# Attention with its largest scores taken ahead, and 3x3 depthwise convolutions shared between TensorE and VectorE

## The chip, the cores and the metric

The kernel runs on one core of a Trainium2 chip. A core has five engines that run on their own and wait for one another by semaphores: TensorE (PE, with its weight loads as PEld), VectorE (DVE), ScalarE (ACT), GpSimd (POOL) and SyncE (SP), whose queue issues most transfers. PE writes its results to PSUM, eight banks of 128 x 512 f32[...]. The metric is the device time of one execution in microseconds (us). The time before is 16835.43 us, the median of three runs (16829.09 to 16853.61).

## The reference

A network of four layers on an input of 4 batches x 96 channels x 56 x 56; each layer adds its result for the normalised input (groups of three channels) to the input.

- Layer 0: attention over all 3136 positions with three heads of 16 channels; softmax over all positions, projection to 96 channels.
- Layer 1: input projection to 192 channels, a 3x3 depthwise convolution, SiLU, and a selective scan along eight paths over the picture (rows, columns and two diagonals, each both ways); the eight results are merged, normalised, gated and projected.
- Layer 2: for each position the eight most similar positions in a window, a weighted mean of them, and a feed-forward net.
- Layer 3: again projection and depthwise convolution, a cumulative recurrence in four directions, a gate, and then a bottleneck: 1x1 convolution to 384 channels, affine and ReLU, a 3x3 depthwise convolution, affine and ReLU, 1x1 convolution to 96, and a squeeze gate over the channels.

For the change, these lines matter:

```python
attn = jnp.einsum('bhnd,bhmd->bhnm', q, k) * scale
attn = jax.nn.softmax(attn, axis=-1)
out = jnp.einsum('bhnm,bhmd->bhnd', attn, v)
...
xc = lax.conv_general_dilated(xc, conv_w, (1, 1), 'SAME', feature_group_count=DI, ...)
xc = jax.nn.silu(xc + conv_b[None, :, None, None])
...
t = jax.nn.relu(bn(conv2d(t, c2_w, c2_b, groups=2 * E, pad=1), bn2_g, bn2_b, bn2_m, bn2_v))
```

## The kernel before

All data are f32. A matmul of f32 leaves two records in the trace[...].

**Layer 0** (`layer0`, L113 to L341). The 3136 positions are cut into 7 chunks of 448 columns (`NCH`, `CH`) and 25 tiles of 128 rows (`NT`, the last of 64). A head has 16 channels, padded to 32, so that the four batches lie in the four strips of 32 partitions (`rows[b]`). `project` (L171) makes queries and keys of one head for one chunk, `values` (L155) the values.

The softmax needs the largest score of each query first. A **unit** (head, tile of queries, chunk of keys) computes the scores (`scores`, L197) of 128 queries against 448 keys for each batch, and `largest` (L210) reduces each on DVE to one maximum per query. When the seven chunks of a tile are done, `of_tile` (L218) takes the maximum of the seven, and `into_row` (L227, L229) turns it into a row and subtracts it within the queries, in a channel that is kept for it. A **step** (head, chunk of 448 queries, tile of 128 keys) then computes the transposed scores (`weigh`, L237), takes the exponential on ACT (`exps`, L246), and sums values and weights in `gathered` (L255): for each batch a matmul over 128 keys into a strip of 32 partitions of one PSUM bank `acc`. After 25 steps, `finish` (L260) copies `acc` (L264), turns the denominators into rows (L267, L269), takes reciprocals in four parts (L273) and multiplies; for the last head it also multiplies by the output weights (L287), adds bias and input (L291) and writes the chunk out (L292).

The order is written out by hand: `in_order` (L53) makes each engine follow the program's order. There are 525 units and 525 steps. 32 units (`LEAD`) go ahead of the first step. Then each step does, twice: weigh two batches, score the other two for a unit, exponentials of the first two (one instruction each), maxima of the other two, sums of the first two. So units and steps advance at one rate, and the last 32 steps have no unit. PSUM: four banks for `weigh` (`psE`), three for everything else (`psM`, `bank()`), one for `acc`.

**Convolutions.** `into_scan` (L344, layer 1), `into_layer3` (L938) and `bottleneck` (L1412, within `layer3`) each fill a padded tile of 128 channels x 58 x 58 (`xp`, `t1`): a projection on PE in seven chunks, each copied by ACT (L385, L972, or with affine and ReLU L1426). `depthwise` (L418) then runs nine instructions on DVE over the whole tile of 128 x 3136: the first multiplies (L423), the others multiply and add in place (L425). ACT applies SiLU or affine and ReLU to the whole tile (L391, L978, L1433). In `into_scan` the result is written to DRAM in four orders: rows as it is; columns through a transposing copy on ACT (L403); the two diagonals through a doubled copy `dup` (ACT L394 and POOL L395) and two gathering copies on POOL (L405, L407). `into_scan` and `into_layer3` have six tiles each (two pairs of batches x three), the bottleneck three for each of four batches. There is no order by hand here; the tile framework places instructions by their dependencies. A pair's inputs are loaded through one buffer `x` (L365, L957) and normalised just before its tiles.

Layer 3's output alternates for each batch between `gathered` (L1374: loads the four directions' results, sums, normalises, gates) and `bottleneck`. Their SBUF pools are opened and closed in turn, so they use the same places: `ob`, `os` for the one, `tb`, `t1`, `ts` for the other.

**Between them** lie the scans (L427 on), layer 1's output, layer 2 and the cumulative sums (L989 on), which the diff doesn't touch.

Of the kernel before, what the change touches and what calls it, by code (L numbers as in the profile page):

```python
# [17 lines left out]
L = H * W  # L18
# [51 lines left out]
class Net:  # L70
# [42 lines left out]
    def layer0(self, xin, xout):  # L113


        nc, tc = self.nc, self.tc
# [4 lines left out]
        LEAD = 32  # L121
        with ExitStack() as cx:
# [4 lines left out]
            psE = cx.enter_context(tc.tile_pool(name="l0pE", bufs=4, space=PSUM))  # L127
# [27 lines left out]
            def values(b, t0):  # L155
                some = n128[t0 : t0 + 8]
                n = some[0][1]
                p = psE.tile([128, 512], F32, name="s")
                for i, (k0, nk) in enumerate(some):
                    nc.tensor.matmul(  # L160
                        p[:nk, i * 48 : (i + 1) * 48], xns[b][:, k0 : k0 + nk], wv, start=True, stop=True
                    )
                nc.scalar.copy(
                    va[:n, t0 : t0 + len(some), :, b, 0:HD],
                    p[:n, : 48 * len(some)].rearrange("p (t h d) -> p t h d", h=HEADS, d=HD),
                )
# [23 lines left out]
            def scores(u, bs):  # L190

                h, t, kc = u
                q0, nq = n128[t]
                ps = []
                for b in bs:
                    p = bank()
                    nc.tensor.matmul(  # L197
                        p[:nq, :CH], qas[h][rows[b], q0 : q0 + nq],
                        kas[h][rows[b], kc * CH : (kc + 1) * CH], start=True, stop=True,
                    )  # L200
                    ps.append(p)
                return ps

            def largest(u, bs, ps):
# [4 lines left out]
                for b, p in zip(bs, ps):  # L209
                    nc.vector.tensor_reduce(  # L210
                        pms[h, t][:nq, b : b + 1, kc], p[:nq, :CH], AX.X, ALU.max
                    )

            def of_tile(u):

                h, t, _ = u
# [5 lines left out]
            def into_row(u):  # L222

                h, t, _ = u
# [6 lines left out]
            def weigh(s, bs):  # L231
# [3 lines left out]
                for b in bs:  # L235
                    p = sc[s, b] = psE.tile([128, 512], F32, name="s")
                    nc.tensor.matmul(  # L237
                        p[:nk, :CH], kas[h][rows[b], k0 : k0 + nk],
# [3 lines left out]
            def exps(s, bs):  # L242
                nk = n128[s[2]][1]
                for b in bs:
                    e = ss.tile([128, CH], F32, name="e", bufs=8)
                    nc.scalar.activation(e[:nk], sc[s, b][:nk, :CH], AF.Exp, scale=scale)  # L246
                    sc[s, b] = e

            def gathered(s, bs):
                h, qc, t = s  # L250
                nk = n128[t][1]
                if t == 0 and bs[0] == 0:
                    sc["acc"] = psA.tile([128, 512], F32, name="acc")
                for b in bs:
                    nc.tensor.matmul(  # L255
                        sc["acc"][rows[b], :CH], va[:nk, t, h, b, :], sc[s, b][:nk],
                        start=t == 0, stop=t == NT - 1,
                    )

            def finish(h, qc):  # L260
# [23 lines left out]
                for b in range(B):  # L284
                    p = bank()
                    for i in range(HEADS):
                        nc.tensor.matmul(  # L287
                            p[:C, :CH], wo[rows[b], i, :], aos[i][rows[b], cs],
                            start=i == 0, stop=i == HEADS - 1,
                        )  # L290
                    nc.vector.scalar_tensor_tensor(xs[b], p[:C, :CH], bo, xs[b], ALU.add, ALU.add)  # L291
                    nc.gpsimd.dma_start(xout[b][:, cs], xs[b])  # L292
                    yield

            with in_order(tc):
                for c in range(NCH):
                    project(0, c)
                parts = [(b, t0) for t0 in range(0, NT, 8) for b in range(B)]
                sc = {}
                at_u = 0  # L300
                ended = None
                done = iter(())
                for at in range(-LEAD, len(steps)):
                    u = units[at_u] if at_u < len(units) else None
                    at_u += 1
                    s = steps[at] if at >= 0 else None
                    new = steps[at + 1] if -1 <= at < len(steps) - 1 else None
                    if s is None and parts:
                        values(*parts.pop(0))
                    for two, first in (((0, 1), True), ((2, 3), False)):  # L310
                        other = (2, 3) if first else (0, 1)
                        if new is not None:
                            weigh(new, two)
                        if u is not None:
                            ps = scores(u, other)
                        if new is not None:
                            exps(new, two)
                        if u is not None:
                            largest(u, other, ps)
                        if s is not None:  # L320
                            gathered(s, two)
                    if ended is not None:
                        into_row(ended)
                        ended = None
                    if u is not None and u[2] == NCH - 1:
                        of_tile(u)
                        ended = u
                    next(done, None)
                    if s is None:
                        continue  # L330
                    h, qc, t = s
                    if qc == 0 and t == 0:
                        aos.append(s1.tile([128, L], F32, name=f"ao{h}", **({"tag": "xn0"} if h == 2 else {})))
                    if t == NT - 1:
                        done = finish(h, qc)
                        next(done)
                    r = at % (NCH * NT) - (NCH * NT - LEAD - 5 * NCH)
                    if h < HEADS - 1 and r >= 0 and r % 4 == 0 and r < 4 * NCH:
                        project(h + 1, r // 4)
                for _ in done:  # L340
                    pass  # L341


    def into_scan(self, xin, dram, orders):  # L344
# [3 lines left out]
        us = []  # L348
        xs = [dram.tile([C, L], F32, name=f"l1x{b}") for b in range(B)]
        with ExitStack() as cx:  # L350
# [8 lines left out]
            for pr in range(NPAIR):  # L359
                u = [dram.tile([128, NB, L], F32, name=f"l1u{pr}{o}") for o in orders]  # L360
                us.append(dict(zip(orders, u)))
                xn = []
                for half in range(2):
                    x = s1.tile([C, L], F32, name="x")
                    nc.sync.dma_start(x, xin[2 * pr + half])  # L365
                    xh = s1.tile([C, L], F32, name=f"xn{half}")
                    self.group_norm(x, xh, ss, ps, "p")
                    nc.sync.dma_start(xs[2 * pr + half], xh)
                    xn.append(xh)

                def project(col, c):
                    p = ps.tile([128, 512], F32, name="p")
                    for half in range(2):
                        nc.tensor.matmul(
                            p[64 * half : 64 * half + 64, :CH], win[:, col : col + 64],
                            xn[half][:, c * CH : (c + 1) * CH], start=True, stop=True,
                        )
                    return p

                for j in range(NB):  # L380
                    xp = sp.tile([128, H + 2, W + 2], F32, name="xp")
                    self.pad_border(xp)
                    for c in range(NCH):
                        p = project(64 * j, c)
                        nc.scalar.copy(  # L385
                            xp[:, 1 + 8 * c : 9 + 8 * c, 1 : W + 1],
                            p[:, :CH].rearrange("p (h w) -> p h w", w=W),
                        )
                    cv = sp.tile([128, H, W], F32, name="cv")
                    self.depthwise(cv, xp, cw[:, j, :])  # L390
                    nc.scalar.activation(cv, cv, AF.Silu, bias=cb[:, j : j + 1])  # L391

                    dup = sp.tile([128, H, 2 * W], F32, name="dup")
                    nc.scalar.copy(dup[:, :, 0:W], cv)  # L394
                    nc.gpsimd.tensor_copy(dup[:, :, W : 2 * W], cv)  # L395
                    for o in orders:
                        dst = us[pr][o][:, j, :]
                        if o == "rows":
                            nc.sync.dma_start(dst, flat(cv))
                            continue  # L400
                        t = sp.tile([128, W, H], F32, name="t")
                        if o == "cols":
                            nc.scalar.copy(t, view(cv, 0, [[1, W], [W, H]]))  # L403
                        elif o == "diag":
                            nc.gpsimd.tensor_copy(t, view(dup, 0, [[1, W], [2 * W + 1, H]]))  # L405
                        else:
                            nc.gpsimd.tensor_copy(t, view(dup, W, [[1, W], [2 * W - 1, H]]))  # L407
                        nc.sync.dma_start(dst, flat(t))
        return us, xs

    def pad_border(self, xp):
        nc = self.nc
        nc.gpsimd.memset(xp[:, 0, :], 0.0)
# [1203 lines left out]
```

## Time and profile before

| | us |
|---|---|
| median of three runs | 16835.43 |
| profiled execution, its own time | 16926.37 |
| its span | 16924.6 |
| layer 0, to the last output products | 0 to 2439 |
| of which: lead of 32 units / loop with units / rest | 66 to 228 / 236 to 2240 / to 2439 |
| into_scan, to the first scan | 2440 to 2797 |
| scans | 2797 to 9286 |
| layer 1's output, layer 2 | 9293 to 10932 |
| into_layer3 | 10933 to 11215 |
| cumulative sums | 11225 to 16122 |
| layer 3's output, of which a bottleneck some 124 | 16131 to 16915 |

The profile is that of one execution. Its page gives each engine's busy time and share, the span in 40 slices with the busy tenths of each engine and the clock granted to TensorE, and groups of instructions by line. PE's busy time counts pipelined matmuls with modelled ends, so a busy PE is not one at its peak; start-to-start distances on its timeline tell more. A stretch gives the same for a chosen part of the span. The share of the span that the chain of waits spends on lines of this change: PE s L237 6%, PE acc L255 6%, DVE cv L425 3%, PE m L197 1%.

### The profile page before, as it was taken

The numbers are of one execution on the slowest core, as the hardware profiler recorded it, in microseconds if no ns is written. First come the engines' busy times: TensorE is split into PE (matmuls) and PEld (weight loads), VectorE is DVE, ScalarE is ACT, GpSimd is POOL, SyncE is SP. The second block draws the span as 40 slices with busy tenths as digits, with TensorE's granted clock in tenths as the row PEclk, the third lists the DMA queues.
The fourth block names the chain that finished last, engine by engine and source line by source line (L and its number), as shares of the span: only waits on it lengthen the run. The fifth ranks groups of instructions, "written<-read, shape, count | busy, mean of one in ns | idle before, by whom it ended". The sixth has DMA issues, their size and how long they took to land.

```text
span 16924.6 us, 498034 instructions
## 1 busy us (share of the span) xinstructions
PE 13192.5 (78%) x220632; PEld 8680.7 (51%) x220632; DVE 14110.1 (83%) x14839; ACT 12324.2 (73%) x16300; POOL 7670.4 (45%) x4010
## 2 busy tenths in 40 slices
PE   8999983777777777777777677738888888888844
PEld 3222222666666666666665545426665656666622
DVE  5666637999999999999999678768888888888887
ACT  2555435999999999999998235448888888888812
POOL 0000005888888888888887000013333333333300
PEclk7999976999999999999999578869999999999966
DMA  0000004334444443434444910032221222222122
GB/s 14 1 1 1 14 27 149 92 90 95 97 102 107 105 95 93 94 90 103 106 101 98 221 48 6 21 79 50 50 50 48 50 50 50 50 50 49 45 64 66
DMA packets 821388, 1152.29 MB, mean 68 GB/s; under 512 B 309360, under 2 KB 728720, under 8 KB 807456
## 3 DMA queue, kind: packets, MB, share of 16 engines
q1 hardware_dynamic: 760320, 1060.20, 25.8%
q10 hardware_dynamic: 53536, 40.96, 1.1%
q8 instruction: 1734, 28.41, 0.7%
q0 software_dynamic: 5376, 19.27, 0.4%
q14 instruction: 422, 3.46, 0.1%
HBM read 842.93 MB, written 277.18 MB: 66 GB/s over the span
## 4 chain that ended last, share of the span: by engine, by line
PE 31%; DVE 28%; ACT 18%; issue 17%; DMA 3%; POOL 2%; SPq 0%; DVEq 0%; ACTq 0%; POOLq 0%
DVE q L555 16%; PE q L1248 6%; PE s L237 6%; PE acc L255 6%; ACT ht L580 5%; ACT e L543 4%; DVE cv L425 3%; ACT phi L1196 2%; PE z L1188 2%; DVE w L1236 2%; PE y L592 2%; PE t L571 2%; PE t L478 2%; ACT w L1204 1%; PE m L197 1%
## 5 line engine op out<-in xcount | busy, mean ns | idle before, releaser
L535 POOL TENSOR_TENSOR q<-du,bm 128x1792 f32<-128x1792 f32 x1344 | 5348.5, 4027 | 3.1 <-DMA bm<-bc 3.0
L555 DVE TENSOR_TENSOR_SCAN q<-e,state,q 128x448 f32<-128x448 f32 x4608 | 4877.5, 1120 | 150.5 <-ACT e L543 144.1
L543 ACT ACTIVATE e<-dl,na 128x448 f32<-128x448 f32 x5376 | 3354.6, 640 | 167.9 <-DVE q L555 113.9
L592 PE MATMUL y<-ht,cd 128*32 128x64 f32 x75264 | 1841.4, 225 | 1464.6 <-ACT ht L580 1464.1
L571 PE MATMUL t<-ident,q 128*128 128x128 f32 x18816 | 2636.0, 294 | 93.8 <-issue 77.7
L1248 PE MATMUL q<-w,m 32*32 32x192 f32 x52224 | 2579.2, 348 | 115.6 <-DVE phi L1257 66.5
L571 PEld LDWEIGHTS t<-ident,q 128*128 128x128 f32 x18816 | 2401.0, 203 | 326.1 <-issue 204.5
L580 ACT COPY ht<-t 128x896 f32<-128x896 f32 x2688 | 2429.1, 904 | 113.6 <-PE t L571 82.5
L592 PEld LDWEIGHTS y<-ht,cd 128*32 128x32 f32 x75264 | 1403.0, 110 | 1941.5 <-ACT ht L580 1924.1
L1248 PEld LDWEIGHTS q<-w,m 32*32 32x32 f32 x52224 | 1869.4, 113 | 737.8 <-issue 166.9
L1257 DVE TENSOR_TENSOR phi<-q,phi 128x768 f32<-128x768 f32 x1632 | 1513.4, 953 | 550.7 <-PE q L1248 524.3
L210 DVE TENSOR_REDUCE pm<-m 128x1 f32<-128x448 f32 (+1 forms) x2100 | 1211.9, 619 | 807.1 <-PE m L197 800.2
L246 ACT ACTIVATE e<-s 128x448 f32<-128x448 f32 (+1 forms) x2100 | 1027.5, 540 | 1162.3 <-PE m L197 820.6
L1269 POOL TENSOR_TENSOR t<-t 128x384 f32<-128x384 f32 x408 | 407.5, 999 | 2999.2 <-DVE t L1268 2999.2
L1188 PE MATMUL z<-ad,sm 32*32 32x256 f32 x39168 | 1277.8, 391 | 398.5 <-ACT phi L1196 384.3
L1196 ACT COPY phi<-z 128x1536 f32<-128x1536 f32 x816 | 1165.1, 1428 | 536.4 <-PE z L1188 536.2
L1236 DVE TENSOR_TENSOR w<-w,misc 128x3072 f32<-128x3072 f32 x408 | 1365.5, 3347 | 84.8 <-PE misc L1220 47.5
L1204 ACT ACTIVATE w<-phi,lntiny,w_k_rmask 128x3072 f32<-128x3072 f32 x408 | 1203.0, 2949 | 2.6
L1212 ACT ACTIVATE phi<-phi,w_k_nmask 128x3072 f32<-128x3072 f32 x408 | 1165.6, 2857 | 2.4
L197 PE MATMUL m<-ka,qa 32*128 32x448 f32 (+1 forms) x4200 | 1134.0, 612 | 10.5 <-DVE pm L210 10.5
L237 PE MATMUL s<-qa,ka 32*128 32x448 f32 (+1 forms) x4200 | 1111.5, 600 | 0.0
L292 POOL DMA_DIRECT2D x<-xc x28 | 14.5, 517 | 2415.6 <-DVE xc L291 2415.6
(253 smaller groups left out, 17917.3 us busy)
## 6 DMA issues: line engine op xcount, KB each, us to landing
bm<-bc SPq DMA_DIRECT2D x896, 448.0 KB
cm<-cd SPq DMA_DIRECT2D x544, 186.0 KB
l1y<-out SPq DMA_DIRECT2D x672, 96.0 KB
l1y<-out SPq DMA_DIRECT2D x672, 72.0 KB
y<-l1y ACTq DMA_DIRECT2D x224, 168.0 KB
l3y<-y SPq DMA_DIRECT2D x1616, 23.2 KB
w<-l3cr SPq DMA_DIRECT2D x408, 48.0 KB
l3cr<-phi SPq DMA_DIRECT2D x408, 48.0 KB
```

The source lines that it names most:

```text
L237: nc.tensor.matmul(p[:nk, :CH], kas[h][rows[b], k0 : k0 + nk], qas[h][rows[b], qc * CH : (qc + 1) * CH], start=True, stop=True,)
L535: nc.gpsimd.tensor_tensor(q, spread(s["du"][:, j, :], ng), s["bm"][g], ALU.mult)
L543: nc.scalar.activation(e[:, :CH], s["dl"][:, j, :], AF.Exp, scale=na[:, s["k"], j, n : n + 1])
L555: nc.vector.tensor_tensor_scan(a, e, a, first, ALU.mult, ALU.add)
L571: nc.tensor.transpose(flat(t)[:, 128 * c : 128 * c + 128], view(q, h * NC2 + c, [[NC, 128]]), self.ident,)
L580: nc.scalar.copy(t, flat(s["t", j, g, h])[:, : NC2 * 128])
L592: nc.tensor.matmul(s["y", j][r : r + 32, c // 4, 64 * half : 64 * half + 64], s["cd"][:, half, g, c, :], s["t", j, g, h][:, 128 * i + 64 * ...
L1188: nc.tensor.matmul(z[32 * b : 32 * b + 32, p, dh].rearrange("p n d -> p (n d)"), s["s"][ps_, dh, b, lo : lo + 32], st["ad"][ps_, dh, 8 * h ...
L1196: nc.scalar.copy(st["phi"][:, :, :, 8 * h : 8 * h + 8, :].rearrange("p a b n d -> p a b (n d)"), z.rearrange("p a b n d -> p a b (n d)"),)
L1236: nc.vector.tensor_tensor(st["w"], st["w"], ut, ALU.mult)
L1248: nc.tensor.matmul(qp[bs, n, :DI], st["m"][bs, 4 * q + n, :], st["w"][bs, :, 4 * q + n, :], start=True, stop=True,)
L1257: nc.vector.tensor_tensor(ph, view(st[q], 0, [[256, 4], [32, 6], [1, 32]]), ph, ALU.mult)
```

## The change

Three parts.

1. Layer 0's order. `LEAD` becomes 160 units, done alone before the first step; their scores go two thirds into tiles of two banks and one third into single banks, and one DVE instruction reduces both batches of a two-bank tile. Values and the projection of head 1 are computed between these units. In each step, three batches (not four) advance by one unit: both of one pair beside the first weighing, one of the other pair beside the second. Each batch has a count of its own (`at_u`). `weigh` writes two batches into a tile of two banks (two such tiles), `exps` takes both in one instruction, and `gathered` sums all four batches of the previous step together. `finish` multiplies by the output weights for two batches at a time.
2. `convolve` replaces `depthwise`: for chunk after chunk, taps 0 to 3 are matmuls with diagonal weights (`dg`, made on DVE) into a PSUM bank, taps 4 to 8 are five DVE instructions in place on that bank, and ACT reads the bank. The next tile's fill runs between. All three convolutions use it, in the program's order; two padded tiles are zeroed once and used in turn.
3. Around it: all four inputs are loaded and normalised first; columns are copied chunk by chunk, one tile late; both halves of `dup` are copied by POOL, with one buffer; layer 3's output has three PSUM buffers (not four) for `pn`, one (not two) for `z` and three for the convolution.

The core of the diff:

```diff
-        LEAD = 32
+        LEAD = 160
+        pairs = (0, 1), (2, 3)
...
-            psE = cx.enter_context(tc.tile_pool(name="l0pE", bufs=4, space=PSUM))
+            psE = cx.enter_context(tc.tile_pool(name="l0pE", bufs=2, space=PSUM))
...
+                if len(p.shape) == 2:
+                    nc.vector.tensor_reduce(pms[h, t][:nq, b : b + 1, kc], p[:nq, :CH], AX.X, ALU.max)
+                else:
+                    nc.vector.tensor_reduce(pms[h, t][:nq, b : b + 2, kc], p[:nq, :, :CH], AX.X, ALU.max)
...
-                for b in bs:
-                    p = sc[s, b] = psE.tile([128, 512], F32, name="s")
+                p = sc[s, bs] = psE.tile([128, 2, 512], F32, name="s")
+                for i, b in enumerate(bs):
                     nc.tensor.matmul(
-                        p[:nk, :CH], kas[h][rows[b], k0 : k0 + nk],
+                        p[:nk, i, :CH], kas[h][rows[b], k0 : k0 + nk],
                         qas[h][rows[b], qc * CH : (qc + 1) * CH], start=True, stop=True,
                     )
...
+                e = ss.tile([128, 2, CH], F32, name="e", bufs=6)
+                nc.scalar.activation(e[:nk], sc[s, bs][:nk, :, :CH], AF.Exp, scale=scale)
+                sc[s, bs] = e
...
+                for bs in pairs:
+                    for i, b in enumerate(bs):
+                        nc.tensor.matmul(
+                            sc["acc"][rows[b], :CH], va[:nk, t, h, b, :], sc[s, bs][:nk, i],
+                            start=t == 0, stop=t == NT - 1,
+                        )
...
+                between = [lambda b=b, t0=t0: values(b, t0) for t0 in range(0, NT, 8) for b in range(B)]
+                between += [lambda c=c: project(1, c) for c in range(NCH)]
+                places = 0
+                for n, u in enumerate(units[:LEAD]):
+                    ps = []
+                    for bs in pairs:
+                        if places % 3 < 2:
+                            p = psE.tile([128, 2, 512], F32, name="s")
+                            two = [p[:, 0], p[:, 1]]
+                            ps.append((bs[0], p))
+                        else:
+                            two = [bank() for _ in bs]
+                            ps += zip(bs, two)
+                        places += 1
+                        for b, p in zip(bs, two):
+                            score(u, b, p)
+                    for b, p in ps:
+                        largest(u, b, p)
+                    if ended:
+                        into_row(*ended.pop())
...
+                    if n % 4 == 2 and between:
+                        between.pop(0)()
...
+                for at in range(len(steps) + 1):
+                    new = steps[at + 1] if at + 1 < len(steps) else None
+                    old = steps[at - 1] if at > 0 else None
+                    one_pair, other = pairs if at % 2 == 0 else pairs[::-1]
...
+                    first = [b for b in other if at_u[b] < len(units)]
+                    second = [b for b in one_pair[at // 2 % 2 :][:1] if at_u[b] < len(units)]
+                    for bs, more in ((one_pair, first), (other, second)):
                         if new is not None:
+                            weigh(new, bs)
+                        ps = [bank() for _ in more]
+                        for b, p in zip(more, ps):
+                            score(units[at_u[b]], b, p)
                         if new is not None:
+                            exps(new, bs)
+                        for b, p in zip(more, ps):
+                            largest(units[at_u[b]], b, p)
+                            at_u[b] += 1
+
+                        if old is not None and (bs == one_pair) == bool(first):
+                            gathered(old)
...
+    def convolve(self, tiles, two, sp, ps):
+        nc = self.nc
+        on_pe = 4
+        for j in range(len(tiles) + 1):
+            now = tiles[j] if j < len(tiles) else None
+            old = tiles[j - 1] if j > 0 else None
+            if now is not None:
+                now["xp"] = two[j % 2]
+                dg = now["dg"] = sp.tile([128, on_pe, 128], F32, name="dg")
+                for k in range(on_pe):
+                    nc.vector.tensor_scalar(
+                        dg[:, k, :], self.ident, now["weights"][:, k : k + 1], None, ALU.mult
+                    )
+            for c in range(NCH):
+                if old is not None:
...
+                    p = ps.tile([128, 512], F32, name="d")
+                    q = p[:, :CH].rearrange("p (h w) -> p h w", w=W)
+                    for k in range(on_pe):
+                        nc.tensor.matmul(q, old["dg"][:, k, :], tap(k), start=k == 0, stop=k == on_pe - 1)
+                if now is not None:
+                    now["fill"](c, now["xp"][:, 1 + 8 * c : 9 + 8 * c, 1 : W + 1])
+                if old is not None:
+                    for k in range(on_pe, 9):
+                        nc.vector.scalar_tensor_tensor(q, tap(k), w[:, k : k + 1], q, ALU.mult, ALU.add)
+                    old["ended"](c, q)
...
+            with in_order(tc):
+                last = []
+                for b in range(B):
+                    normalise(b)
+                self.convolve([tile_of(pr, j) for pr in range(NPAIR) for j in range(NB)], two, sp, ps)
+                last[0](tuple(range(NCH)))
...
-            ps = cx.enter_context(tc.tile_pool(name="op", bufs=4, space=PSUM))
-            psz = cx.enter_context(tc.tile_pool(name="oz", bufs=2, space=PSUM))
+            ps = cx.enter_context(tc.tile_pool(name="op", bufs=3, space=PSUM))
+            psz = cx.enter_context(tc.tile_pool(name="oz", bufs=1, space=PSUM))
+            psd = cx.enter_context(tc.tile_pool(name="od", bufs=3, space=PSUM))
```

## The prediction

> **What bounds the kernel now.** I read the page's sums and slices first, then stretches of the four places that the diff touches, then timelines inside them. From the page (engine sums, slices of 423 us, granted clock):
> ```profile
> PE 13192.5 (78%) x220632; PEld 8680.7 (51%) x220632; DVE 14110.1 (83%) x14839; ACT 12324.2 (73%) x16300; POOL 7670.4 (45%) x4010
> ...
> PE   8999983777777777777777677738888888888844
> ...
> DVE  5666637999999999999999678768888888888887
> ...
> PEclk7999976999999999999999578869999999999966
> ```
> The first six slices, layer 0, have a PE at 9 and a DVE at 6: here PE decides. The next and the last two slices have DVE far above PE. Stretches by stage (span, then busy PE, PEld, DVE, ACT, POOL, then clock): lead, loop and tail of layer 0, into_scan, into_layer3, one bottleneck.
> ```profile
> 66.00:228.00 162.00, 151.50 (x443) 85.74 (x443) 71.28 (x130) 7.80 (x17) 0.00 (x0) 0.51 0.00 0
> 241.00:2240.00 1999.00, 1998.42 (x12328) 524.22 (x12330) 1253.94 (x2241) 989.02 (x2015) 10.39 (x20) 1.00 0.02 4
> 2300.00:2420.00 120.00, 120.00 (x276) 26.06 (x274) 2.04 (x3) 31.47 (x65) 1.54 (x3) 0.50 0.03 10
> 2440.00:2797.00 357.00, 60.24 (x196) 24.61 (x196) 250.59 (x108) 106.95 (x80) 105.03 (x41) 0.56 0.39 148
> 10933.00:11215.00 282.00, 51.22 (x184) 22.05 (x184) 202.48 (x106) 83.32 (x64) 2.38 (x22) 0.56 0.40 99
> ...
> 16206.00:16330.00 124.00, 61.24 (x154) 30.07 (x154) 91.97 (x33) 31.51 (x43) 1.24 (x12) 0.71 0.13 29
> ```
> The loop has no idle PE and a full clock; lead and tail run at half clock. PE's timeline shows what a half step consists of (start, length, line, tile, records; a matmul of f32 leaves two records):
> ```profile
> 1005.57 0.64 PE L237 MATMUL s<-qa,ka 32*128 32x448 f32 x2
> 1005.59 0.65 PE L197 MATMUL m<-ka,qa 32*128 32x448 f32 x2
> 1006.05 0.54 PE L237 MATMUL s<-qa,ka 32*128 32x448 f32 x2
> 1006.07 0.54 PE L197 MATMUL m<-ka,qa 32*128 32x448 f32 x2
> 1006.54 0.94 PE L255 MATMUL acc<-e,va 128*32 128x448 f32 x4
> 1007.41 0.64 PE L237 MATMUL s<-qa,ka 32*128 32x448 f32 x2
> ```
> Four score matmuls lie in four row strips at once: 0.97 us (1005.57 to 1006.54). Only two sums lie in column strips: 0.87 us. Half a step is 1.84, a step 3.68. Between 850 and 1275 us 442 maxima (line 210, four per step) ran, so a step took 3.85 on average; the 0.17 are turned tiles (L227), reciprocals and L264.
>
> **The skill.** The Trainium skill, TensorEngine Tiling, "Key Properties", says that a change of tiling mode drains TensorE. The trace agrees: back-to-back records in one mode start 0.375 us apart (below), across a change 0.47. TensorE: Matmul & The Clock Gate, Part 1, has two clocks, half and full, by how busy PE was; this trace shows 0.50 and 1.00. SBUF — State Buffer, "Who interferes with whom", says that a DVE instruction with two SBUF inputs waits for a GpSimd one that reads SBUF, one with a single SBUF input does not. Its first half shows in into_scan on GpSimd's and on DVE's timeline: the copy and the tap take 8.77 and 8.45 us side by side, 5.7 and 3.48 alone:
> ```profile
> 2536.90 8.77 POOL L405 COPY t<-dup 128x3136 f32<-128x3136 f32 x1
> ```
> ```profile
> 2540.50 8.45 DVE L425 SCALAR_TENSOR_TENSOR cv<-xp,w_l_cw,cv 128x3136 f32<-128x3136 f32 x1
> ```
>
> **Layer 0, loop.** Sums of all four batches go out together: one column block per step, not two, so 0.87 and two mode changes go. The scores form two row blocks: two weighing and two maximum scores, then two and one. The second block lies against the next step's first without a mode change, where records follow at 0.375:
> ```profile
> 1757.45 2.12 PE L287 MATMUL m<-ao,w_l_wo 32*96 32x448 f32 x5
> ```
> (first gap 0.45, then 0.375 each). So a step is 0.97 + 0.87 + 2 x 0.375 = 2.59 us. The three-strip block saves nothing, since strips run side by side. Is anything else slower? DVE: three maxima at 0.58 (L210: two take 1.16) plus 0.2 of rest, 1.95. ACT: two exponentials of 128x896; L580's copy of that size from PSUM is 0.904, so 1.81. The maximum of block one is ready at 1.0, done at 2.15; its banks are wanted at 2.6: 0.45 spare. The pair tile of the exponentials, two deep, is free at 1.95, wanted at 2.6. So PE remains the bound, with little spare. Overhead: turned tiles come 3 in 28 steps, not 1 in 7, so 0.17 becomes 0.13; for each turned tile shifting the ring of three banks and for reciprocals (0.8 us) ahead of a maximum I add 0.08. Step 2.80 (ends: 2.65 with no such waits, 3.10 if the 0.45 is too little each step).
> 365 units x 4 batches at 3 per step take 487 steps: 487 x 2.80 = 1364 us. project(2): seven times eight matmuls, two modes' change, 2.2 us: 15. Output products L287 in pairs: per chunk two pairs x six records x 0.375 = 4.6, five chunks before the tail: 23. Last 38 steps without maxima: PE 0.97 + 0.87 = 1.84 against ACT 1.81 plus a handover, 2.0: 76, and 9 for one chunk. The end, 2423 to 2439 now, 14.
>
> **Layer 0, lead.** 160 units alone instead of 32. DVE: of six pairs of maxima four are one instruction over two banks (448 elements cost 0.535 start to start; L1267 and L1268, 1536 in 1755 ns and 768 in 958, give 1.04 ns an element, so 896 cost 1.0 us), two are single pairs (1.07): 6.14 us for three units, and 0.08 for turned tiles: 2.13. At half clock a score takes 1.86 us to be ready and the two-bank round trip 3.03 equals DVE's 3.07, so any PE work between shows: 12 values at 3.7 us (16 records at 0.213 each), 4 small at 0.6, 7 project(1) at 3.4: 71; 22 into_row at 0.6: 13. 160 x 2.13 + 84 = 425 (at full clock 370). No view shows which clock it gets; I take half, as in the lead of before.
> Sum: 66 + 425 + 1364 + 15 + 23 + 85 + 14 = 1992 against 2439: **447 saved** (350 to 560).
>
> **Convolutions.** Now DVE does nine taps per tile, 1.8 + 8 x 3.40 = 29 us. After: four on PE, per chunk of 448 eight records x 0.375 = 3.0, plus the fill (0.75 and a mode change in layers 1 and 3's input: 3.95 per chunk, 27.7 per tile; 1.5 in the bottleneck: 4.5, 31.5). DVE: five per chunk; 96x448 of this kind at L1462 starts every 0.59 us, no row shows one writing PSUM; between 0.59 and 0.70, I take 0.62: 21.7 per tile, 24 with the wait. ACT's three copies per chunk are 2.1. PE is the bound, so a tile costs what it did; what is won is that fills, Silu and copies run beside it. The diagonals, 4 per tile at some 0.2, fall before GpSimd's copies start.
> into_scan: loads of four inputs, four norms at 8.3 us (2467.6 to 2475.9 is one): 50; first fill 10; five tiles at 28, the last 23; GpSimd's four copies (L395 2.8, L407 5.6) 17, then the queue of SP and loads, 29 as now: 269 against 357: **88 saved** (20 to 120). DVE's taps have one SBUF input and should not wait for GpSimd; if they do, 17 us per tile come back.
> into_layer3: 50 + 10 + 140 + 23 + 14 = 237 against 282: **45 saved** (10 to 70).
> Bottleneck: first fill 15 at half clock, two tiles 31.5, last 22.5, c3's rest 9: 110 against 120 (16206 to 16326). But the next batch's loads start when the pool of t1 and cv is free, 3 us after the last tap, and hide under c3 and gate:
> ```profile
> 16299.74 10.53 DVE L425 SCALAR_TENSOR_TENSOR cv<-t,w_l_c,cv 128x3136 f32<-128x3136 f32 x3
> ```
> ```profile
> 16313.36 0.32 SPq L1377 DMA_DIRECT2D xn<-l3x  x1
> ```
> ```profile
> 16324.91 0.96 DVE L1395 TENSOR_TENSOR y<-y,y 112x768 f32<-112x768 f32 x1 [14.65 <-DMA y<-l3y]
> ```
> After, that pool holds only diagonals (4 KB); xn and y then lie where x and t2 lie, which are read to the batch's end. So loads come some 27 us later, three times: 81 less 40: **40 lost** (60 lost to 50 saved if the places don't overlap). psz with one buffer: the next z is wanted some 8 us of DVE later and takes 2.6: nothing.
>
> **Sum.** -447 - 88 - 45 + 40 = -540 on a profiled execution of 16926 us (span 16925), which lies 91 above the runs' median. 16835 - 540 = **16295 us**; its own range 16210 to 16380.
>
> **Rivals.** (a) Clock and waits turn out kind: lead at full clock (-55), steps at 2.65 (-73), loads not late: about 16140. For it: the loop's clock is 1.00 throughout. Chance 0.20. (b) Bank handover takes the place of the removed block: maxima return their three banks too late, step 3.10: +146, 16440. For it: the spare of 0.45; against: DVE only 70% busy. Chance 0.20. (c) The convolutions don't pay, DVE's taps waiting for GpSimd or for PSUM: +150, 16445. Chance 0.10. (d) Slower: PE falls to half clock in the loop, as in the tail of before, where one row block took 1.69 and one column block 1.64. A step would be 1.69 + 1.5 + 1.64 + 0.3 = 5.1, 525 x 2.3 = 1200 more: 17500. It decides from a step of 2.80 + 540/487 = 3.91 on. Against it: eleven matmuls in 2.6 us are denser than twelve in 3.68, which hold full clock. 0.03. (e) No change, the lead paying back all: a lead of 965 us; 0.02.
> The forecast itself has 0.45. 16120 to 16460 leaves out the far parts of (a), (b), (c) and (d). About 0.2% is what a measurement can tell: faster 0.96, same 0.01, slower 0.03.
>
> **What would show it.** Right: sums in groups of eight records, a step near 2.8 us and DVE near 70% in the loop; layer 0 ending near 1990; lead to near 490; PE at 8 or 9 in the convolutions, the taps on DVE near 0.62 apart; the load of xn in layer 3 after the last output. Wrong if maxima wait (PE idle before scores), if taps on DVE are over 0.75 or grow beside GpSimd, or if clock is 0.5 in the loop.

## The result and the profile after

The changed kernel takes 16559.86 us (median of 4 runs, 16535.73 to 16583.74) against 16837.03 us for the kernel before in the same runs: a ratio of 0.9834, 95% interval 0.9816 to 0.9852. It is faster by 277 us. The forecast of 16295 named the direction and almost twice the size, and the time lies outside its range. The profiled execution took 16544.92 us, its span is 16543.1.

The page after, PE's busy tenths in slices of 414 us and the granted clock:

```profile
PE   8999977777777777777776678778888888888866
...
PEclk6899889999999999999998588889999999999977
```

In the last two slices, layer 3's output, PE now stands at 6 where it stood at 4. But in layer 0 the clock's row lacks the steady 9 of before: it shows 8 in slices 2 and 5. Stretches (us, then busy PE, PEld, DVE, ACT, POOL, then clock): the lead; the loop's first 25 steps; steps 25 to 175; head 2's chunks with output products, steps 375 to 475; steps 475 to 500; into_scan; into_layer3.

```profile
66.00:485.00 419.00, 411.62 (x1626) 199.27 (x1624) 336.24 (x469) 15.95 (x31) 0.00 (x0) 0.56 0.00 1
...
485.00:617.00 132.00, 131.78 (x590) 35.41 (x588) 48.99 (x87) 48.86 (x55) 0.00 (x0) 0.70 0.00 1
617.00:1044.00 427.00, 427.00 (x3348) 155.71 (x3344) 292.36 (x518) 265.60 (x306) 0.00 (x0) 1.00 0.01 1
...
1652.00:1993.00 341.00, 333.36 (x2328) 120.75 (x2324) 205.00 (x360) 178.28 (x204) 8.33 (x16) 0.95 0.06 17
1993.00:2128.00 135.00, 132.79 (x498) 32.95 (x494) 26.63 (x47) 44.74 (x51) 2.05 (x4) 0.65 0.04 11
...
2202.00:2478.00 276.00, 184.87 (x532) 76.39 (x532) 175.89 (x288) 96.23 (x141) 104.51 (x34) 0.82 0.52 193
10602.00:10838.00 236.00, 176.54 (x520) 73.55 (x520) 175.11 (x286) 88.14 (x132) 0.77 (x8) 0.86 0.44 113
```

Steps 25 to 175 are as forecast: full clock, DVE busy 68%, a median step of 2.60 us, a mean of 2.85. The rest of the loop is not: stretches at clock 0.70, 0.65 and, for steps 225 to 275, 0.91, and one at 0.95 with 3.41 us per step. The places where the time went, predicted and as the two traces show them:

| place | predicted | the two traces |
|---|---|---|
| layer 0, to the end of its outputs | -447 | 2439 to 2202: -237 |
| into_scan | -88 | 357 to 276: -81 |
| into_layer3 | -45 | 281 to 236: -45 |
| layer 3's output | +40 | 783 to 802: +19 |
| places that the diff doesn't touch | 0 | -38 |
| sum | -540 | -382 |

Layer 0 is what failed. PE's timeline between 506 and 556 us has a step as it was costed, and two others:

```profile
507.18 0.96 PE L251 MATMUL acc<-e,va 128*32 128x448 f32 x8
508.07 0.65 PE L233 MATMUL s<-qa,ka 32*128 32x448 f32 x2
508.08 0.95 PE L196 MATMUL m<-ka,qa 32*128 32x448 f32 x2
...
509.78 0.96 PE L251 MATMUL acc<-e,va 128*32 128x448 f32 x8
...
519.40 0.96 PE L251 MATMUL acc<-e,va 128*32 128x448 f32 x8
...
521.14 0.92 PE L233 MATMUL s<-qa,ka 32*128 32x448 f32 x4
521.99 0.97 PE L196 MATMUL m<-ka,qa 32*64 32x448 f32 x4
522.89 0.96 PE L251 MATMUL acc<-e,va 128*32 128x448 f32 x8
...
545.79 1.72 PE L251 MATMUL acc<-e,va 128*32 128x448 f32 x8
547.45 1.86 PE L233 MATMUL s<-qa,ka 32*128 32x448 f32 x4
549.24 1.75 PE L196 MATMUL m<-ka,qa 32*64 32x448 f32 x2
...
554.40 1.72 PE L251 MATMUL acc<-e,va 128*32 128x448 f32 x8
```

At 508 weighing (L233) and maximum scores (L196) start within 0.02 us of each other in different row strips, and the step lasts 2.60. At 521 the units have reached the last tile, of 64 queries: its scores are 32*64 and start 0.85 us after the weighing ones, not beside them, and a step takes 3.49. A little later the clock falls, each block takes 1.7 to 1.9 us, and the step takes 8.61 (545.79 to 554.40). Every head has its last tile once.

### The profile page after: what moved, and what is told of

It is laid out like the page before. It is cut to its first block, busy times and chain, and to the rows that moved or that the text cites. A ratio compares the mean times of both kernels' runs of the same rounds, so it can differ in the third digit from the quotient of the medians.

```text
span 16543.1 us, 501276 instructions
## 1 busy us (share of the span) xinstructions
PE 13366.7 (81%) x221976; PEld 8983.6 (54%) x221976; DVE 13918.8 (84%) x15345; ACT 12240.4 (74%) x15452; POOL 7665.0 (46%) x3968
## 3 DMA queue, kind: packets, MB, share of 16 engines
q14 instruction: 425, 3.48, 0.1%
## 4 chain that ended last, share of the span: by engine, by line
PE 32%; DVE 28%; ACT 19%; issue 15%; DMA 5%; SPq 1%; POOL 1%; DVEq 0%; ACTq 0%; POOLq 0%
DVE q L638 17%; PE q L1357 7%; ACT ht L663 5%; PE s L233 4%; ACT e L626 3%; PE d L417 3%; ACT phi L1305 3%; DVE w L1345 3%; PE z L1297 2%; PE acc L251 2%; PE m L196 2%; ACT w L1313 2%; PE t L561 2%; PE y L675 2%; DVE phi L1366 2%
## 5 line engine op out<-in xcount | busy, mean ns | idle before, releaser
L241 ACT ACTIVATE e<-s 128x896 f32<-128x896 f32 (+1 forms) x1050 | 921.7, 915 | 902.6 <-PE m L196 508.2
L208 DVE TENSOR_REDUCE pm<-m 128x1 f32<-128x448 f32 (+1 forms) x1672 | 982.9, 616 | 667.1 <-PE m L196 599.6
L196 PE MATMUL m<-ka,qa 32*128 32x448 f32 (+1 forms) x3344 | 1169.3, 638 | 7.5 <-DVE pm L208 7.5
L1297 PEld LDWEIGHTS z<-ad,sm 32*32 32x32 f32 x39168 | 708.7, 104 | 659.6 <-ACT phi L1305 463.0
```

Source lines behind the costliest of these rows:

```text
L1297: nc.tensor.matmul(z[32 * b : 32 * b + 32, p, dh].rearrange("p n d -> p (n d)"), s["s"][ps_, dh, b, lo : lo + 32], st["ad"][ps_, dh, 8 * h ...
```

## Experiments

The kernel before, run beside each group of experiments, had medians from 16837 to 16864, so kernels of different groups are compared by their ratios to it; 0.001 is 17 us. Most intervals are 0.002 to 0.003 to each side, and its own times scatter differently from group to group (e12), so a saving between groups is known to some 30 us; where medians and ratios differ, both are given.

**The last tile's queries filled up (e1).**

```diff
-                    qas.append(s1.tile([128, L], F32, name="qa", bufs=2))
+                    qas.append(s1.tile([128, NT * 128], F32, name="qa", bufs=2))
+                    nc.vector.memset(qas[h][:, L:], 0.0)
...
-                    p[:nq, :CH], qas[h][rows[b], q0 : q0 + nq],
+                    p[:, :CH], qas[h][rows[b], q0 : q0 + 128],
```

> The changed kernel; queries lie in 3200 columns, the last 64 of them zero, so that the last tile's scores also use 128 columns of the array instead of 64 (their extra rows are not read). Theory 1 (the score matmuls of 32x64 cannot run beside the weighing ones of 32x128, the row blocks fall apart, and TensorE then drops to half clock): no stretch of the loop at clock 0.5, no steps of 8.6 us; layer 0 ends about 140 us earlier, near 2065, and the time is 16420 (16400 to 16450). Rival (the clock falls in these stretches for another reason, for instance the time since the loop began, or the waits for banks): the steps of 8.6 us stay and the time is 16560 within 15.

Measured: 16444.78 us, ratio 0.9748 (0.9719 to 0.9778), so 115 us less by the medians, 145 by the ratios. The last sum of layer 0 ends at 2039.8 instead of 2187.3. The same tile, in PE's timeline of e1:

```profile
520.00 0.96 PE L252 MATMUL acc<-e,va 128*32 128x448 f32 x8
520.89 0.65 PE L234 MATMUL s<-qa,ka 32*128 32x448 f32 x2
520.91 0.94 PE L197 MATMUL m<-ka,qa 32*128 32x448 f32 x2
...
522.60 0.96 PE L252 MATMUL acc<-e,va 128*32 128x448 f32 x8
```

and the stretch of its first 25 steps:

```profile
484.00:556.00 72.00, 72.00 (x570) 25.84 (x566) 46.04 (x83) 44.80 (x52) 0.00 (x0) 1.00 0.00 1
```

The same 25 steps take 72 us at full clock where they took 132 at 0.70, and the last ones 81 instead of 135. More multiplications, less time: theory 1 holds. By mean steps the three stretches gave 53, 28 and 55 us, 136 of the 148; 9 more are the lead, which ended sooner in this execution. Two things are in the 136. In these stretches the clock's records show half clock for 198 us in the changed kernel and for 10 in e1. A block takes 0.9 us at full clock and 1.7 to 1.9 at half, so half of the difference, some 94 us, is an estimate of what the fallen clock cost. The remaining 42 or so are blocks that no longer lie side by side.

**Keys and values filled up too (e2).**

```diff
-                    kas.append(s1.tile([128, L], F32, name="ka", bufs=2))
+                    kas.append(s1.tile([128, NT * 128], F32, name="ka", bufs=2))
+                    nc.vector.memset(kas[h][:, L:], 0.0)
...
-                            sc["acc"][rows[b], :CH], va[:nk, t, h, b, :], sc[s, bs][:nk, i],
+                            sc["acc"][rows[b], :CH], va[:, t, h, b, :], sc[s, bs][:, i],
```

Weighing, exponentials and sums then take 128 keys in every step; the values' rows beyond the last key are zero.

> As e1, and keys and values of the last tile filled up to 128 too (values zero there), so that the step of 64 keys has no 32x64 and no 64x32 matmul. Theory 1: that step falls from 3.81 us to 2.6 in each of 21 chunks, 25 us below e1, 16395. Rival (that step is long because the sum's bank is copied before the next chunk, as every chunk's end): the same as e1 within 8 us.

Measured: 16405.38 us, ratio 0.9722 (0.9697 to 0.9748), 39 below e1, more than theory 1 had. But it had the wrong step: the gap of 3.81 us stays, so it belongs to the chunk's end, as the rival says. (In e2's trace this step also holds the denominators' matmul, L266, of 1.02 us, just after the copy of the sums; how much of the gap is either was not tested.) What shrank are two of the steps before it, from 3.70 to 2.60 and from 3.48 to 2.60 (4.46 to 3.62 where a turned tile falls there). The mean of steps 25 to 175 went from 2.85 to 2.77, 2.0 us per chunk, 41 for 21 chunks. From the first group of sums to the last the two traces differ by 27 only (1553 and 1526): e2 spent 20 us more at half clock among head 2's output products (58 against 38; e5 and e6), which by the same estimate takes back some 10.

**The same filling of queries in the kernel before (e3).**

> The kernel before, with the queries filled up as in e1. Theory 1: there one weighing and one maximum score per half step lie beside each other in pairs of batches; in the three stretches of 25 steps with the last tile a step takes 4.5 us instead of 3.86, so 30 to 50 us are saved: 16795. Rival (those steps are long for another reason): 16837 within 15. In either case the last tile costs this kernel a third of what it costs the changed one, since its clock holds.

Measured: 16817.03 us, ratio 0.9974 (0.9964 to 0.9985), 39 to 44 saved, as theory 1 says. The kernel before paid for the last tile too, but a third of what the changed one pays: its clock stayed at 1.00 through the loop. What e3 saves is near the 42 us that e1 leaves beside the clock.

**The convolutions alone (e4), the attention alone (e11).** e4 is the changed kernel with `layer0` of before, e11 the kernel before with the new `layer0`.

> The convolutions' part of the change alone, with the attention of before. If the parts add up as the two traces show by stage: 81 + 45 - 19 = 107 us below before, 16730, and the attention's part is the other 170 to 237. If the convolutions gain nothing of their own on the median (the trace of before being a slow one): above 16790.

> The attention's part of the change alone, with the convolutions of before. Theory (the saving of 237 us between the two traces contains some 60 us that only the profiled execution of before had: its sums after the loop ran at half clock, 2296 to 2477 us, while in e4, with the same code, they ran at full clock and ended 62 us earlier): the part is worth 277 - 94 = 183, ratio 0.989, 16675. Rival (the 237 are real and the convolutions' part is worth less beside it): 16620, ratio 0.986.

Measured: e4 16771.94 us, ratio 0.9944 (0.9923 to 0.9966), some 94 us (84 by the medians; a little short of the 107 expected); e11 16661.72, ratio 0.9898 (0.9881 to 0.9914), some 172 (181 by the medians). They add up to 265 of the 277 to 280, so within the scatter the parts are independent, the rival of e11 falls, and layer 0 is worth far less than the 237 of the two traces. In e4, `layer0` of before ended its last sum at 2360.6 us, in the trace of before the same code at 2422.9. The new `layer0` scatters as well: its last sum ends at 2187.3 in the changed kernel, at 2182.3 in e7 and at 2161.8 in e11.

**The kernel before, profiled again (e12).**

> The kernel before, unchanged, profiled a second time. Theory: the clock of the sums after layer 0's loop is not the same in every execution; here the stretch from 2240 us to layer 0's end is at full clock as in e4 and the span is 16840 to 16870. Rival: half clock again, the last sum at 2422, span near 16925.

Measured: 16844.71 us (one execution), span 16842.9, last sum at 2359.8. The stretch of the tail (the clock is the third number from the end) in this execution,

```profile
2296.00:2420.00 124.00, 87.42 (x359) 27.58 (x358) 23.83 (x40) 38.52 (x77) 4.44 (x15) 0.81 0.23 64
```

and in the one of before that was read for the prediction:

```profile
2296.00:2420.00 124.00, 124.00 (x285) 26.94 (x286) 2.27 (x4) 32.72 (x67) 2.05 (x4) 0.50 0.04 11
```

The loops ahead of it are alike (PE busy 1998.42 of 1999 us in both, at 1.00); the tail, which has no maxima beside the sums, ran at half clock in the one execution and not in the other. That is 63 of the 82 us between the two. Three more traces with this tail (e3, e4, e10) have it at full clock. It may be less rare than one in five: of 60 timed executions of the kernel before, beside the result and the experiments, 46 took 16826 to 16880 us and 14 took 16899 to 16924, a gap of about this size. Only the one of 16926 has a trace, so that the 14 had the same tail is not shown.

**The output products of head 2 (e5, e6).** After e2, steps with L284's products (L287 in e2's numbering) were the longest left. In the changed kernel PE does this:

```profile
1667.21 2.05 PE L284 MATMUL m<-ao,w_l_wo 32*96 32x448 f32 x10
1668.73 0.64 PE L196 MATMUL m<-ka,qa 32*128 32x448 f32 x1
...
1669.46 0.92 PE L233 MATMUL s<-qa,ka 32*128 32x448 f32 x4
1671.15 1.01 PE L196 MATMUL m<-ka,qa 32*128 32x448 f32 x2 [0.77 <-DVE pm L208]
```

e5 fills the output weights to 128 columns (`wo8[rows[b], i, :]` in the place of `wo[rows[b], i, :]`). e6 leaves the weights and takes away the yield between products and additions:

```diff
-                    yield
                     for b in bs:
                         x = xs[b]
                         nc.vector.scalar_tensor_tensor(x, p[b % 2][:C, :CH], bo, x, ALU.add, ALU.add)
```

> e2 with the output projection's weights filled up to 128 columns by zeros (the extra rows are not read), so that these products are 32x128 like the scores around them. In e2 four to five steps per chunk of head 2 are long (6.63, 4.21, 5.91, 5.08, 4.24 us instead of 2.6), together some 80 us, where 23 were predicted. Theory M (the 32x96 products cannot lie beside the 32x128 scores, so the row blocks fall apart as with the last tile): 30 to 60 us below e2, 16360, and no half clock around 1740 and 1820 us. Theory B (the pair of products holds two of the three banks until its additions, so scores wait): the same as e2 within 10 us, 16405.

> e2 with the additions to the output products issued in the same step as the products, not one step later, so that their two banks come back sooner. Theory B (banks): 30 to 60 us below e2, 16360. Theory M (modes): within 10 us of e2, or slower, since the maxima then wait on VectorE behind the additions.

Measured: e5 16383.74 us, ratio 0.9717, 8 below e2 by the ratio, 22 by the medians, and within the interval the same; e6 16357.28, ratio 0.9700, 37 below e2 by the ratio, 48 by the medians. The intervals of e2 and e6 overlap, so the steps decide. In the first chunk with products e5 has 6.65, 4.21, 5.91, 5.08, 4.24 us, as e2 to within 0.02: at full clock the form 32*96 was not the cause, and there theory M falls. Whether the form bears on the clock stays open: from step 375 to 500 e5 spent 17 us at half clock, e2 58 and e8, with the same products as e2, 85. e6 has 5.88, 5.87 and then 2.60: steps 375 to 475 went from 3.43 to 3.00 on average, layer 0's last sum from 2021.6 to 1971.9, and this stretch of e6 is at full clock:

```profile
1541.00:1841.00 300.00, 299.85 (x2328) 113.24 (x2324) 204.72 (x361) 177.16 (x205) 8.33 (x16) 1.00 0.07 20
```

The sums of successive steps in that chunk begin, in e2, at

```profile
1556.42 0.96 PE L254 MATMUL acc<-e,va 128*32 128x448 f32 x8
...
1563.05 0.96 PE L254 MATMUL acc<-e,va 128*32 128x448 f32 x8
...
1567.26 0.96 PE L254 MATMUL acc<-e,va 128*32 128x448 f32 x8
```

and in e6:

```profile
1554.19 0.96 PE L254 MATMUL acc<-e,va 128*32 128x448 f32 x8
...
1560.07 0.96 PE L254 MATMUL acc<-e,va 128*32 128x448 f32 x8
...
1565.94 0.96 PE L254 MATMUL acc<-e,va 128*32 128x448 f32 x8
...
1568.54 0.96 PE L254 MATMUL acc<-e,va 128*32 128x448 f32 x8
```

So scores waited for the two of three banks that a pair of products held for another step. In e2's steps 375 to 475 PE stands idle for scores behind the maxima of the third bank for 6.1 us in all, in e6's never; the rest of the gain is scores that lie side by side again, and up to half of e2's 58 us at half clock. What is left in e6 is twice 3.28 us per chunk, 6.6 where 4.6 were predicted.

**The pools of layer 3's output apart (e7, e10).**

```diff
             for b in range(B):
                 g = ga.tile([96, 2, L], F32, name="g")
-                with ExitStack() as c2x:
-                    sp = c2x.enter_context(tc.tile_pool(name="ob", bufs=1))
-                    ss = c2x.enter_context(tc.tile_pool(name="os", bufs=3))
-                    gathered(b, g, sp, ss)
+                gathered(b, g, ob, os)
```

with `ob` and `os` opened ahead of the loop. e7 is the changed kernel with this edit, e10 the kernel before with it.

> The changed kernel with the pools for the inputs of layer 3's output stage made once ahead of the loop over batches, so that they share no place with the bottleneck's tiles. Theory (the next batch's loads wait for the last reader of x, as the trace has it: loads issued at 15931.2, 16132.7 and 16332.0, when the last output of the batch before ends; VectorE then idles 11 us for the first load, and 31 us lie between its last tap and its first addition, 15 in the kernel before): loads come during the taps, 31 us become a few, three times: 50 to 90 us below the changed kernel, 16490. Rival (the loads are only the last of several waits; tensors of outputs and norms fill the gap anyway): less than 20.

> The kernel before with e7's edit. Theory (it was the change that made the loads late: in the kernel before they are issued 3 us after the last tap, and VectorE idles 15 us for them, where it idles 31 in the changed kernel; the rest hides under outputs): 30 to 45 us saved in three times, ratio 0.9977. Rival (the loads were as costly before, and e7's gain is nothing of the change's): 90 to 110 us saved, ratio 0.994.

SP's issues and DVE in the changed kernel at a batch's end,

```profile
15931.36 0.31 SPq L1487 DMA_DIRECT2D xn<-l3x  x1
```
```profile
15930.54 0.68 DVE L1576 SCALAR_TENSOR_TENSOR o<-t,gate,x 96x448 f32<-96x448 f32 x1 [0.83 <-DMA out<-o]
15942.33 0.96 DVE L1505 TENSOR_TENSOR y<-y,y 112x768 f32<-112x768 f32 x1 [11.11 <-DMA y<-l3y]
```

and in e7, where the same batch's last tap comes at 15937.78 and its last output ends at 15959.6:

```profile
15827.54 0.32 SPq L1487 DMA_DIRECT2D xn<-l3x  x1
```
```profile
15952.96 0.96 DVE L1505 TENSOR_TENSOR y<-y,y 112x768 f32<-112x768 f32 x1 [0.19 <-DMA y<-l3y]
```

Measured: e7 16477.56 us, ratio 0.9767 (0.9746 to 0.9788), 82 us below the changed kernel by the medians, 113 by the ratios; e10 16805.67, ratio 0.9969 (0.9954 to 0.9983), some 52 (58 by the medians). The distance between last outputs of batches fell from 201, 199, 200 to 165, 164, 159 us in e7, and from 192, 192, 187 (e12) to 174, 171, 163 in e10. In the traces that makes 114 and 63, more than expected: in e7 the next batch's gating (L1512) and additions (L1505) also run between the outputs. Of e7's 114, 63 could have been had before; 51, or 17 per transition, is put down to the later loads of the change. The run times give 82 to 113 against 52 to 58, so 24 to 61 for the same difference. With pools apart, the new convolutions save 7 us per batch (e7's distances against e10's).

**A shorter lead (e8), and all together (e9).** e8 is e2 with `LEAD = 152`; e9 is e2, e6, e7 and e8 in one.

> e2 with 152 units alone instead of 160. A unit alone takes 425 / 160 = 2.65 us; in the loop the same unit takes 4/3 of a step that would be needed anyway and grows from 2.42 to 2.77 us. So 8 x 2.65 = 21 us less lead and 4 more loop: 17 below e2, 16388. Rival (the lead ends in work that has to be done alone anyway: values and projections that are put among its units): within 6 of e2.

> e2's filled tiles, e6's additions at once, e8's 152 units alone and e7's pools apart, in one kernel. If the gains add up (e2 155, e6 37, e8 15, e7 82 to 113 below the changed kernel or below e2): 16230 (16200 to 16270). Rival (part of them is one gain counted twice, for instance by a clock that holds anyway): over 16290.

Measured: e8 16390.19 us, ratio 0.9713, 15 below e2, as expected but within the interval. Its lead ended 23 us sooner, its last sum only 6: the loop is 17 longer, of which 4 were expected, and 14 are by the estimate above its 85 us at half clock against e2's 58. e9 takes 16237.96 us (5 runs), ratio 0.9619 (0.9597 to 0.9641): 3.8% below before, more than twice the gain of the change as it stood. The gains add up, as expected. Its loop's stretch:

```profile
472.00:1960.00 1488.00, 1485.06 (x11760) 551.14 (x11759) 985.42 (x1744) 931.29 (x1080) 12.43 (x24) 1.00 0.02 7
```

## Why the prediction was wrong in size

**What bounds it, and the cost of a step.** Right. Sums go in groups of eight, the median step is 2.60 (2.59 worked out), and PE is the bound.

**What failed** is the next line of the working, "487 x 2.80 = 1364": it took the commonest kind of step for all of them. About ten steps per head have a 64-query unit beside them. There the two kinds of scores differ in form and no longer lie in four strips at once: 3.5 to 5.0 us per step at full clock, and 8.61 where the clock fell. This cost some 136 us in the traces, 115 to 145 in the run times (e1). The Trainium skill's sentence on modes (TensorEngine Tiling, "Key Properties": a change of tiling mode drains TensorE) had been applied to the two kinds of block that were shown, not to the last tile; and in the trace of before the same tile's steps were long already (most of them 5.4 us where others take 3.7), which its mean of 3.85, taken from 850 to 1275 us, left out.

**The term for 64 keys** was missing as well: 39 us (e2).

**Output products**, 23 predicted for five chunks. In e2, where nothing else disturbs them, the excess over 2.6 in the first of these chunks is 13 us, and two later ones at half clock reach 22 and more. With the additions at once the products cost 6.6 per chunk against 4.6 (e6); that they hold two of three banks across a step was not seen. It is rival (b)'s mechanism, in five places instead of in every step: 50 us between the traces of e2 and e6, part of it the clock.

With these three repaired, layer 0's last sum ends at 1972 (e6). The prediction's 1992, less its 14 for the end, is 1978. The lead holds (to end near 491; it ended at 485, at a mean clock of 0.56), and so does project(2): steps 175 to 225 take 12 us more than the steps around them, against 15. The tail was too cheap by 16 (its steps are 2.10 and 2.65 by turns, 2.42 on average and not 2.0), and the step of e2 and e6, 2.77 against 2.80, gives that back, so that 1972 meets 1978 partly by errors that cancel.

**The convolutions.** into_scan and into_layer3 hold: 81 and 45. Taps start 0.72 to 0.73 us apart within a chunk (0.79 a few times), not 0.62 and just past the stated end of 0.70, but PE hides the difference (chunks of 4.11 against 3.95, in the bottleneck 4.51 against 4.5). Beside GpSimd's copies they don't stretch, as the Trainium skill has it (SBUF — State Buffer, "Who interferes with whom", for a DVE instruction with one SBUF input): all 420 taps of layers 1 and 3's inputs last between 680 and 692 ns, the 109 with a copy of GpSimd beside them among them. For layer 3's output the mechanism held as written: the load of xn comes when the last output ends. Its size was some 17 us per transition (e7, e10), not 27, which left 19 lost, not 40.

**The sum.** It was worked out against the profiled execution of 16926 us and then taken from the median, with 91 us between them. But 63 of these were half clock in the very tail that the change replaces: a saving that the median does not hold. Against the second trace of before, layer 0's last sum moved from 2360 to 2187, 173 us, and e11 gives 172 to 181. So of the 265 us by which the forecast fell short, 210 are layer 0's terms, less 21 for the output of layer 3 and plus 7 for into_scan; the rest, some 68, is the choice of the execution (91 and the 15 by which the trace after lies below its median, less 38 in untouched places).

**Rivals.** (d), half clock in the loop, came true in places: 18 steps of 8.6 us or more, not everywhere. (Its 1.69 us was read from a block of 32*64 in the trace of before; the block of 32*128 at 2411.11 took 1.79.) (b) came true in five chunks. (c) fell. None of them named the last tile, and their sizes, each set against the forecast alone, were not added, so the range of 16460 missed by 100 us.

## What to carry to other kernels

When a step's cost rests on matmuls lying side by side in strips, cost the odd tile (the last, shorter one) by itself: filling it up with zeros was free here and worth some 1% of the whole time. A ring of three buffers must be counted over the whole time that the rarest user holds them, a step's end included. And before a difference of traces is taken from a median, look whether the profiled execution differs from the median in the very stretch that the change removes.

## What the runs showed of the hardware

In the trace of the changed kernel, none of the 168 records of 32*64 maximum scores ran beside a 32*128 weighing one in another row strip: two matmuls of the one form and two of the other took 0.9 us each, one pair after the other, where four of one form lie side by side in 0.97 together. The 6 that did start within 0.02 us of a weighing one started beside those of the last 64 keys, which are 32*64 too.

After a few such steps the clock fell to 0.50 and stayed there for 31 to 96 us, although PE was busy throughout by the profile's count (131.78 of 132 us). With the strips filled it stayed at 1.00 for 1488 us (e9). So this busy time alone did not hold the clock; which measure of work does was not tested.

The clock of one and the same code can differ from execution to execution: the tail of the kernel before, 2296 us on, had half clock in one of five traces and full clock in four.
